# A planned graph network kernel: loads on ScalarE's queue, a third layer's product in three passes, one addition on GpSimd alone

## The chip, the cores and the metric

The kernel runs on one core of one Trainium2 chip. The metric is device microseconds of one execution, the median of several runs. The changed kernel is compared with the kernel before on the same inputs. Engine names in the profile: PE is TensorE (matmuls), PEld is its weight load, DVE is VectorE, ACT is ScalarE, POOL is GpSimd, SP is SyncE, which only issues transfers. PEq, ACTq, SPq and so on are the queues of instructions of these engines. L992 is line 992 of the kernel.

## The reference, cut to what matters

There are 128 graphs of 128 nodes with 256 features each, and an adjacency matrix of 0 and 1 for each graph. Four layers follow each other. Each normalises x, takes the positive part, computes a graph layer and adds the result to x.

```python
h = relu(layernorm(x))
# layer 0: three steps of a gated recurrent cell, the weights shared by the steps but for weight[i]
for i in range(3):
    aggr = A^T @ (h @ weight[i])                  # A = (adj != 0)
    gi, gh = aggr @ w_ih.T + b_ih, h @ w_hh.T + b_hh
    r, z = sigmoid(gi_r + gh_r), sigmoid(gi_z + gh_z)
    n = tanh(gi_n + r * gh_n)
    h = (1 - z) * n + z * h
x = x + h
# layer 1: for each relation r, (adj == r) @ h @ weight[r], summed, plus a bias
# layers 2 and 3: graph attention
e = leaky_relu(ei[:, None] + ej[None, :], 0.2)    # ei, ej: two projections of h @ W
x = x + softmax(where(adj, e, far)) @ (h @ W)
```

All arrays are float32. Adjacency values above 1 would need more than one relation in layer 1. The kernel holds a second program for that case and picks one at run time; with these inputs it takes the program for values 0 and 1.

## The kernel before

**Groups.** The work goes in 32 groups of four graphs (`G = 4`, `NG = 32`). A tile of one group is 128 partitions by 512 columns. Several groups are in flight at once, and x of a group is read twice, once for layer 0's normalisation (`load`, L529) and once at the last step of layer 0 (`fetch` at L1090), because only three buffers hold x. The adjacency tile is read three times for a group: at `load`, as its transpose (L1095), and in `again` (L522) for the masks of layers 2 and 3.

**Layer 0.** For each step, `step` (L940) forms three float32r pieces of h and of the aggregate (`forms`, L948): a rounded high part (L955 on ACT or L957 on DVE), a low part (L961, DVE), and their difference (`difference`, L468, on POOL or DVE). The gates are then sums of matmuls of 128x512 (`products`, L985, matmul L992) in three passes; between the second and the third pass the bank in PSUM is scaled by 1 + 2^-12 (`rescale`, L1003: L1013 on ACT or L1011 on DVE; L1005 scales with a bias). L1023 and L1040 are the tanh of the gates, L1035 to L1048 the elementwise updates on DVE. The new h is turned by `turn` (L478): a transpose in 32x32 blocks on DVE (L490), a write to DRAM (L493) and four reads back (L502). After the last step, two tiles of h are added to x (`residual`, L1078), on DVE or on POOL, whichever the planner finds free.

**Layers 1 to 3.** `product` (L792) computes a pair of graphs: first the sums over neighbours (`sums`, L761, matmul L765), then the product with the weights. A layer named in `THIN` does the second part in float32r in three passes: the sums are rounded to a high part (L806 on ACT, L808 on DVE), a low part follows (L811, DVE), a difference (L470), two passes (L819), a scale of the bank (L828 on DVE, L830 on ACT) and the third pass (L819). The three pieces lie in one set of buffers, `cform`. A layer that is not in `THIN` copies the sums (L461, on ACT or DVE) and does a plain float32 product (`mix`, L771, matmul L775). The last two groups (`PLAIN = 2`) are always plain. Before the change `THIN` is `(1, 2)`: the weights of layer 3, `wa_1`, are kept as plain float32 and those of layers 1 and 2 in three pieces, made at the start by `split` (L573). In the profile both `wa_0` and `wa_1` are written `wa`, since buffer numbers are left out.

**The start.** Weights come in, are split into pieces (L580 to L586) and, for layer 0, multiplied together (L598). All adjacency tiles are read once (L668) and their maximum taken (L670) to choose the program; all engines branch at L1236.

**What sets the order.** A planner (`Plan`, L172) records every operation with its engine or choice of engines, a cost, and the buffers it reads and writes. `order` (L215) then plays the operations forward in its own time: of those that can start on an engine soonest it takes the one with the lowest rank, and for an operation with two engines it settles which one. A rank is made of the group's due time (`PERIOD`, `CLOSE`), the length of the way behind the operation, and a number of its own from the table `OFFSETS`, one for each place in the code and stage. `LAG`, `HOP`, `OWN` and the argument `late` say when a result is seen by another engine. The order that comes out is fixed in the program; every engine works through its own list in order, and an instruction that waits holds those behind it.

Transfers are planned like operations of the engine that issues them. In the kernel before all of them but the first four weights are issued by SP:

```python
op("SP", dma(256), lambda g2=g2: nc.sync.dma_start(
    out=xt.t[:, 2 * g2 : 2 * g2 + 2, :],
    in_=x[ds(gi * G + 2 * g2, 2)].rearrange("g n d -> n g d")),
   w=[(xt, {2 * g2, 2 * g2 + 1})], after=after)
```

Transfers of both queues take turns with eight completion semaphores, so each also waits for the one eight issues before it.

Of the kernel before, what the change touches and what calls it, by code (L numbers as in the profile page):

```python
# [15 lines left out]
ALU = mybir.AluOpType  # L16
AX = mybir.AxisListType

P = 128
D = 256  # L20
KC = D // P
G = 4
T = G * P
# [15 lines left out]
OWN = {"PE": 0, "ACT": 125, "DVE": 125, "POOL": 80, "SP": 2500, "ACTQ": 2500}  # L39
PERIOD = 29902  # L40
CLOSE = 7183
CLOSING = 2
SOON = -210
# [3 lines left out]
LINE, SPREAD = 0, -1000  # L47
GIVE = -400
TAKE = -2500
TENSOR = ()  # L50
BLOCK = 32
NEAR = 69
# [12 lines left out]
THIN = (1, 2)  # L65
# [11 lines left out]
def act(n, ptrs=0):  # L77
    return 50 + 95 * ptrs + 0.833 * n


def dve(n):
    return 68 + n / 0.96


def dma(kb):
    return 470
# [3 lines left out]
    0: (-70252, -12514, 2287, 8809, -26238, -146194, 10750, 55634, 30994, -54821, -2879, -215, -254,),  # L90
    1: (-77596, -18751, -40109, -33244, -13055, -53723, -68528, 1773, -34806, -135119, 879, -98768, 51856,
        44795, -64452, -2716,),
    2: (-95804, -20611, 70568, -66959, -6282, -38365, 6331, 7167, -87557, -120685, 144159, 0, -60172, 22200,
        253, 2907, 38047,),
    3: (-102445, -23990, 38859, 16506, -38395, -77755, 61821, 576, 58832, 37279, 38392, 48590, -137270, -161,
        -4329, 88294, -5659, -1511, -24936, -35483,),
    4: (9420, 6970, 96990, 45577, 14137, -3081, -28597, -108133, -850, -77398, -8748, -81, 24213, -39147,
        5274, -117520, -39070, 4328, 73461, 2677, -9322, 38218,),
    5: (-53063, -10484, 13614, 9709, -9223, 0, 86360, -49387, 3891, -79089, 22834, -12125, 42, -143071,
        -20815, -7001, 39402, 8197, 210921, 979, -8129, 55104, -109511, 178418, -171023, -17919, -45955,  # L100
        32785, 202299, 15929, -75290, -16189,),
    6: (-8401, 1876, 0, -2867, -17545, -54409, -177384, 6635, -4173, 16809, 64025, 1422, -41374, 3498, 7298,
        112681, -960, 0, -167733, 3047, -20901, 48681, -50794, 104147, -14530,),
    7: (2011, -43268, -7473, -2193, -13120, 17374, 10030, 24727, -8835, -59753, 29500, -32772, -10542,
        -85496, -6214, -47593, 4322, -5746, -43839, -101654, -3101, 9392, -18883,),
    10: (31340, 140410, 166041, 86764, 86271, -82403, 47762, 173067, 157481, -33091, 90840, -8460, 85813,),
    11: (-90811, -5747, -11338, -10756, 2168, -27498, -36330, -9110, 13623, -65824, 59954, -36485, 65854,
        102114, -39462, 10659,),
    12: (-88894, -2718, 120398, -47746, 16864, -33143, 17060, 25017, -58235, -111482, 170409, 89873, -65258,
        61044, 3422, 23111, 49690,),  # L110
    13: (-59071, 17894, 109447, 41927, -4268, -51312, 111328, 77067, 108356, 88471, 46360, 263340, -35253,
        23414, 79162, 211888, 10834, -10383, 74698, 67176,),
    14: (-32758, 12684, 122607, -43352, -20519, -34186, -56784, -88737, -18648, -122741, -24236, -29303,
        31876, -49287, -17477, -128202, -71886, 71670, 64769, 11212, -103569, -34527,),
    15: (-186417, -106904, -40789, -64266, -8033, -13445, 16411, -115394, -129609, -221523, -34547, -153159,
# [258 lines left out]
def kernel(  # L374
# [20 lines left out]
    nc = tc.nc  # L395
# [28 lines left out]
    def build(general):  # L424
# [3 lines left out]
        op = plan.op  # L428
# [49 lines left out]
        def turn(nm, srcs, dst=None, w=None):  # L478
# [27 lines left out]
            return w  # L506

        state = {}

        def fetch(gi, name, after=()):  # L510
            xt = Buf(xs, f"{name}{gi}")
            for g2 in range(G // 2):
# [772 lines left out]
```

## Time and profile before

| what | value |
|---|---|
| median of 3 runs | 2353.08 us (2349.69 to 2353.46) |
| profiled execution, its own time | 2353.06 us |
| its span, first to last instruction | 2351.2 us |
| granted TensorE clock, mean | 0.996 |
| bytes moved over the span | 270.36 MB, 115 GB/s |
| matmuls of layer 0's gates (L992) | 6912 |
| issues on SP's queue: x loads, adjacency loads | 128; 96, and 32 more for the maximum |

In the lines of the profile's groups, the order is: line, engine, operation, tile written and tiles read, shapes, count; then busy time in us, mean length of one in ns; then the idle time just before them, and what ended most of it. In a line of waits, the numbers are the total in us, how many times, and the longest. In a timeline they are the start in us and the length. A busy sum of a TensorE line counts the time in which one of its matmuls was under way; neighbouring lines overlap.

### The profile page before, as it was taken

What the parts mean: (1) busy time and instruction counts of PE and PEld (TensorE: products, weight loads), DVE (VectorE), ACT (ScalarE), POOL (GpSimd) and SP (SyncE); (2) the same over time, 40 slices, a digit from 0 to 9 for tenths busy, and PEclk for the clock granted to TensorE, in tenths of its full rate; (3) what the DMA queues carried; (4) which work ended last, traced back from release to release, by engine and by line L of the source; (5) the groups of instructions that cost most, each with busy time, mean ns of one, the idle gap of its engine ahead of it and who ended that gap; (6) DMA issues with size and microseconds to landing.
All of it is one profiled execution on the core that took longest, in us unless ns stands there. A gap on an engine that the chain in (4) does not pass through costs nothing.

```text
span 2351.2 us, 39064 instructions
## 1 busy us (share of the span) xinstructions
PE 2291.9 (97%) x12137; PEld 1947.2 (83%) x12137; DVE 1978.2 (84%) x5405; ACT 1582.0 (67%) x3272; POOL 912.4 (39%) x729
## 2 busy tenths in 40 slices
PE   7999999999999999999999999999999999999997
PEld 6788888888888888888888888888888888788885
DVE  7858888888888888888888888888888888888887
ACT  6566676766676666666666766666766666666665
POOL 2334334443334443334343334343334343344421
PEclk9999999999999999999999999999999999999999
DMA  8535445555445455455455455455554555545431
GB/s 249 143 83 110 96 90 124 117 128 116 102 110 125 111 133 113 100 117 117 114 126 118 107 115 115 114 129 116 108 115 112 118 122 109 128 103 118 105 77 43
DMA packets 951273, 270.36 MB, mean 115 GB/s; under 512 B 677008, under 2 KB 939280, under 8 KB 951056
## 3 DMA queue, kind: packets, MB, share of 16 engines
q1 hardware_dynamic: 949968, 266.72, 50.0%
q8 instruction: 99, 1.62, 0.3%
q14 instruction: 118, 0.97, 0.2%
q10 hardware_dynamic: 1088, 1.05, 0.1%
HBM read 168.96 MB, written 98.69 MB: 114 GB/s over the span
## 4 chain that ended last, share of the span: by engine, by line
PE 64%; DVE 14%; DMA 10%; ACT 6%; SPq 4%; issue 3%; DVEq 0%; POOL 0%; ACTq 0%
PE bank L992 40%; PE bank L819 7%; PE bank L765 6%; PE bank L974 5%; PE bank L775 5%; DMA swap<-big 4%; SPq L502 4%; DMA big<-swap 3%; DVE junk L1119 3%; DVE form L961 2%; DMA wide<-swap 2%; ACT big L743 1%; DVE wide L1042 1%; DVE wide L1045 1%; DVE big L490 1%
## 5 line engine op out<-in xcount | busy, mean ns | idle before, releaser
L992 PE MATMUL bank<-form,wh_s 128*128 128x512 f32 x3456 | 953.4, 396 | 8.7 <-ACT bank L1005 4.6
L992 PE MATMUL bank<-form,wi_s 128*128 128x512 f32 x3456 | 944.0, 393 | 1.6 <-ACT bank L1013 0.9
L470 POOL TENSOR_TENSOR form<-form,form 128x512 fp32r<-128x512 f32 x383 | 517.7, 1362 | 800.4 <-DVE form L961 565.0
L992 PEld LDWEIGHTS bank<-form,wi_s 128*128 128x128 f32 x3456 | 644.1, 188 | 143.6 <-ACT bank L1013 3.1
L992 PEld LDWEIGHTS bank<-form,wh_s 128*128 128x128 f32 x3456 | 631.8, 188 | 151.5 <-ACT bank L1005 15.8
L1013 ACT ACTIVATE bank<-bank 128x512 f32<-128x512 f32 x448 | 255.4, 574 | 325.7 <-PE bank L992 324.4
L722 POOL TENSOR_TENSOR small<-small,nhalf 128x4 f32<-128x4 f32 (+2 forms) x140 | 142.2, 1020 | 408.8 <-DVE small L720 338.9
L1119 DVE CUSTOM_DVE_ANT_0 junk<-big,ub 128x256 bf16<-128x256 f32 x512 | 244.5, 478 | 14.2 <-ACT big L743 0.5
L743 ACT ACTIVATE big<-xs,small 128x256 f32<-128x256 f32 x384 | 200.1, 590 | 21.6 <-DVE small L726 12.2
L696 DVE BATCH_NORM_STATS2 small<-xs 128x6 f32<-128x256 f32 x512 | 190.0, 415 | 7.3 <-DMA xs<-in_x_dram 6.0
L470 POOL TENSOR_TENSOR cform<-cform,cform 128x512 fp32r<-128x512 f32 x120 | 155.2, 1294 | 96.2 <-DVE cform L811 83.0
L490 DVE STREAM_TRANSPOSE big<-wide 128x512 f32<-128x512 f32 x252 | 173.1, 697 | 4.0 <-ACT wide L743 2.3
L1035 DVE SCALAR_TENSOR_TENSOR bank<-big,bank 128x512 f32<-128x512 f32 x192 | 131.9, 690 | 48.5 <-PE bank L992 35.9
L955 ACT ACTIVATE form<-wide 128x512 fp32r<-128x512 f32 x179 | 109.2, 626 | 83.7 <-DMA wide<-swap 43.4
L1179 ACT ACTIVATE big<-big,small 128x128 f32<-128x128 f32 x256 | 99.8, 392 | 70.0 <-DVE small L1173 69.7
L1023 ACT ACTIVATE bank<-bank,b_rz 128x512 f32<-128x512 f32 x192 | 123.4, 655 | 34.0 <-PE bank L992 30.1
L1210 DVE SCALAR_TENSOR_TENSOR xs<-bank,small,xs 128x256 f32<-128x256 f32 x256 | 118.4, 475 | 31.6 <-PE bank L775 23.0
L1042 DVE TENSOR_TENSOR wide<-wide,bank 128x512 f32<-128x512 f32 x192 | 126.9, 682 | 21.4 <-ACT bank L1040 21.1
L765 PE MATMUL bank<-big,big 128*128 128x128 f32 x1024 | 130.7, 277 | 11.9 <-DVE wide L1045 7.1
L1023 ACT ACTIVATE big<-bank,b_rz 128x512 f32<-128x512 f32 x192 | 130.1, 681 | 16.3 <-PE bank L992 12.1
L765 PEld LDWEIGHTS bank<-big,big 128*128 128x128 f32 x1024 | 123.1, 192 | 19.4 <-DVE wide L1045 9.9
L974 PE MATMUL bank<-adjs,big 128*128 128x128 f32 x1024 | 131.2, 276 | 6.4 <-DMA big<-swap 5.1
(105 smaller groups left out, 3297.5 us busy)
## 6 DMA issues: line engine op xcount, KB each, us to landing
swap<-big SPq DMA_DIRECT2D x312, 256.0 KB, 2.5
big<-swap SPq DMA_DIRECT2D x992, 64.0 KB, 2.3
xs<-in_x_dram SPq DMA_DIRECT2D x128, 256.0 KB, 3.1
adjs<-in_adj_dram SPq DMA_DIRECT2D x64, 256.0 KB, 3.4
wide<-swap SPq DMA_DIRECT2D x128, 128.0 KB, 3.6
big<-line SPq DMA_DIRECT2D x60, 256.0 KB, 3.9
out_dram<-xs SPq DMA_DIRECT2D x30, 512.0 KB, 3.1
big<-in_adj_dram SPq DMA_DIRECT2D x32, 256.0 KB, 4.0
```

Of the source, the lines that this page charges most:

```text
L470: (nc.gpsimd if eng == "POOL" else nc.vector).tensor_tensor(at(df), at(lo).bitcast(F32), at(hi).bitcast(F32), ALU.subtract)
L490: nc.vector.transpose(part.t, src())
L696: op("DVE", dve(D), lambda g=g: nc.vector.bn_stats(s.t[:, ST + 6 * g : ST + 6 * g + 6], xt.t[:, g, :]), r=[(xt, {g})], w=[(s, {("mv", g)})])
L743: nc.scalar.activation(place(g), xt.t[:, g, :].rearrange("p (k m) -> p k m", k=KC), AF.Relu, bias=s.t[:, MR + g : MR + g + 1], scale=s.t[: ...
L765: nc.tensor.matmul(ps.t[:, (len(gs) * k + j) * P : (len(gs) * k + j + 1) * P], hs[g // 2].t[:, (g % 2) * D + k * P : (g % 2) * D + (k + 1) ...
L819: nc.tensor.matmul(po.t[:, j * D : (j + 1) * D], fs[f].t[:, (len(gs) * k + j) * P : (len(gs) * k + j + 1) * P], w.t[:, f, k, :], start=(st ...
L974: nc.tensor.matmul(pg.t[:, g * P : (g + 1) * P], of()[:, g * P : (g + 1) * P], flags(m0)[:, g * P : (g + 1) * P], start=True, stop=True,)
L992: nc.tensor.matmul(ps.t, w.t[(slice(None), *row, j, k, slice(c * P, (c + 1) * P))], b.t, start=(start and x == 0), stop=(x == len(terms) - ...
L1013: nc.scalar.mul(ps.t, ps.t, by)
L1023: op("ACT", act(T, 1), lambda: nc.scalar.activation(to.t, ps.t, AF.Tanh, bias=b_rz.t[:, c : c + 1], scale=0.5), r=[b_rz, *([ps] if kept el ...
L1042: op("DVE", dve(T), lambda c=c, ps=ps: nc.vector.tensor_tensor(hT.t[:, c, :], hT.t[:, c, :], ps.t, ALU.subtract), r=[ps], w=[(hT, {c})])
L1119: nc.vector.tensor_tensor_reduce(out=junk.t, in0=part, in1=ub[i].t[:, v, :], op0=ALU.mult, op1=ALU.add, scale=1.0, scalar=0.0, accum_out=s ...
```

## The change

1. The loads of x and of the adjacency tiles are issued by ACT's queue (`QUEUE = "ACT"`, new function `arrive`); weights, turns, rows of the attention, the reads for the maximum and the stores stay on SP.
2. `THIN` takes in layer 3: its weights are split at the start, and its products go in three passes.
3. The last h is added to x on POOL alone.
4. The planner's numbers are new: an issue costs 530 ns instead of 470 (`ISSUE`), a load on ACT is seen 4400 ns late (`LANDING`), a transfer's own delay `OWN` on SP is 4500 instead of 2500, the costs of `act` and `dve` are some ns higher, `PERIOD`, `CLOSE`, `SOON`, `NEAR`, `GIVE`, `TAKE`, `LINE` and `SPREAD` change, and every number of `OFFSETS`. So every engine's order changes, and which of ACT and DVE does an operation that both can do.

```diff
-OWN = {"PE": 0, "ACT": 125, "DVE": 125, "POOL": 80, "SP": 2500, "ACTQ": 2500}
-PERIOD = 29902
-CLOSE = 7183
+OWN = {"PE": 0, "ACT": 125, "DVE": 125, "POOL": 80, "SP": 4500, "ACTQ": 2500}
+PERIOD = 36849
+CLOSE = 17602
...
-SOON = -210
+SOON = 295
...
-LINE, SPREAD = 0, -1000
-GIVE = -400
-TAKE = -2500
+LINE, SPREAD = -1800, -1400
+GIVE = -2500
+TAKE = -2600
...
+ISSUE = 530
+LANDING = 4400
+QUEUE = "ACT"
...
-NEAR = 69
+NEAR = 19
...
-THIN = (1, 2)
+THIN = (1, 2, 3)
...
-    return 50 + 95 * ptrs + 0.833 * n
+    return 57 + 95 * ptrs + 0.833 * n
...
-    return 68 + n / 0.96
+    return 74 + n / 0.96
...
-    return 470
+    return ISSUE
...
-                op("SP", 470, give, r=[part], w=[(swap, {k})], late=GIVE)
+                op("SP", ISSUE, give, r=[part], w=[(swap, {k})], late=GIVE)
...
-            op("SP", 470 * P // BLOCK, take, r=[swap], w=[w], late=TAKE)
+            op("SP", ISSUE * P // BLOCK, take, r=[swap], w=[w], late=TAKE + 800 * (n - 1))
...
+        def arrive(dst, src, w, after=()):
+            on_act = QUEUE == "ACT"
+            op(QUEUE, dma(256), lambda: (nc.scalar if on_act else nc.sync).dma_start(out=dst(), in_=src), w=w,
+               after=after, late=LANDING if on_act else 0)
...
-                op("SP", dma(256), lambda g2=g2: nc.sync.dma_start(
-                    out=xt.t[:, 2 * g2 : 2 * g2 + 2, :],
-                    in_=x[ds(gi * G + 2 * g2, 2)].rearrange("g n d -> n g d")),
-                   w=[(xt, {2 * g2, 2 * g2 + 1})], after=after)
+                arrive(lambda g2=g2: xt.t[:, 2 * g2 : 2 * g2 + 2, :],
+                       x[ds(gi * G + 2 * g2, 2)].rearrange("g n d -> n g d"), [(xt, {2 * g2, 2 * g2 + 1})], after)
...
-                    def residual(eng, k=k, h=h):
+                    def residual(k=k, h=h):
                         part = xt.t[:, :, k * P : (k + 1) * P]
-                        (nc.gpsimd if eng == "POOL" else nc.vector).tensor_tensor(
-                            part, part, h.t.rearrange("p (g d) -> p g d", g=G), ALU.add)
-
-                    op(("DVE", "POOL"), (dve(T), 1250), residual, r=[h], w=[(xt, set(range(G)))], port=True)
+                        nc.gpsimd.tensor_tensor(part, part, h.t.rearrange("p (g d) -> p g d", g=G), ALU.add)
+
+                    op("POOL", 1250, residual, r=[h], w=[(xt, set(range(G)))], port=True)
```

The adjacency loads in `again`, in `load` and before layer 1 change to `arrive` in the same way; the cost of `terms` (L1125) goes from 850 to 880.

## The prediction

> **What bounds the kernel now.** I read the page's engine totals first, then the busy time in stretches of one period in the middle of the run, then the chain that ended last, then the costs by kind and form, and last the queues and the start.
>
> ```profile
> span 2351.2 us, 39064 instructions
> PE 2291.9 (97%) x12137; PEld 1947.2 (83%) x12137; DVE 1978.2 (84%) x5405; ACT 1582.0 (67%) x3272; POOL 912.4 (39%) x729
> ```
> ```profile
> 1019.30:1090.00 70.70, 70.51 (x378) 60.02 (x377) 61.55 (x165) 48.25 (x101) 28.19 (x23) 1.00 0.53 116
> 1090.00:1160.00 70.00, 69.72 (x377) 59.93 (x377) 60.36 (x165) 48.35 (x101) 28.04 (x23) 1.00 0.52 117
> ```
> After each stretch stand its length and the busy time of PE, PEld, DVE, ACT and POOL, then the granted clock. TensorE is busy 70.5 of 70.7 us and 69.7 of 70.0 us, at full clock. One group of four graphs passes every 70.4 us or so (12 periods from 1019.34 to 1867.22 us: 70.66 each). ACT leaves 22 us of each period free, POOL 42, DVE 9 to 10. So TensorE's own work sets the pace; all 59.3 us of its idle time lie at the ends and in small holes (15.2 us before 60 us, 17.0 after 2280, some 27 between).
>
> The chain gives TensorE's pace as starts that do not overlap (start, length, what):
>
> ```profile
> 1064.38 1.73 PE bank L775 x8
> 1066.10 0.93 PE bank L819 x8
> 1067.04 1.73 PE bank L775 x8
> 1068.76 0.47 PE bank L819 x4
> ```
> L775 is a plain layer 3 product of a pair of graphs: eight records, 1.73 us. L819 is the three-pass form that layers 1 and 2 use: 8 records (two passes) in 0.93 us, 4 (the third) in 0.47.
>
> ```profile
> L470 POOL TENSOR_TENSOR cform<-cform,cform 128x512 fp32r<-128x512 f32 x120 | 155.2, 1294 | 96.2 <-DVE cform L811 83.0 <-DVE small L710 6.8 <-DVE small L711 4.3
> L811 DVE SCALAR_TENSOR_TENSOR cform<-cform,bank 128x512 fp32r<-128x512 f32 x120 | 81.4, 679 | 5.0 <-ACT cform L806 4.9
> L830 ACT ACTIVATE bank<-bank 128x512 f32<-128x512 f32 x97 | 56.6, 583 | 62.0 <-PE bank L819 61.9
> L1080 DVE TENSOR_TENSOR xs<-xs,big 128x512 f32<-128x512 f32 x47 | 40.9, 870 | 69.6 <-DMA big<-swap 66.5 <-issue 3.1
> L1080 POOL TENSOR_TENSOR xs<-xs,big 128x512 f32<-128x512 f32 x13 | 17.1, 1315 | 25.0 <-DMA big<-swap 21.1 <-ACT big L1179 2.8 <-DVE form L961 1.0
> ```
> Here the mean length (ns) after each busy sum prices what is added and moved.
>
> **The change part by part.** Counts are from the order of instructions in the two built programs, first branch of the If (the inputs take it).
>
> **Layer 3 in three passes.** 60 pairs (30 groups; the last two groups keep the plain form) lose 1.73 us and gain 0.93 + 0.47 = 1.40: 60 x 0.33 = 19.8 us less on TensorE, all on the path that sets the end. The busy sums would give less: L775 with wa is 120.8 us for 512 records, of which 480 go (113 us), against 107.6 us for the 720 of L819 with wa, hence 5.7. But those sums overlap at every change of line (the PE rows together pass 2291.9 us by far), so I take the chain's starts and keep 5.7 as the low end. The other engines pay: 60 of L811 (0.679) = 41 us on DVE and 60 differences (1.294) = 78 us on POOL. The copy of the pair's sums becomes the rounding, and one rescale per pair is new.
>
> **What the planner moves between ACT and DVE.** ACT: +77 rescales of the product (0.583) = 44.9, +87 of L1013's kind (0.574) = 49.9, +15 roundings (0.595) = 8.9, -24 of L955 from wide (0.626) = -15.0, -13 copies (0.586) = -7.6, rest some 4: +85 us. DVE: +41 above, -87 L1011 (0.695) = -60.5, -47 copies (0.663) = -31.2, +45 roundings (0.682) = 30.7, -17 rescales (0.700) = -11.9, +24 roundings from wide (0.423) = 10.2, -47 residuals (0.870) = -40.9: -61 us with small change. DVE falls to about 1917 us (82%).
>
> **The last h added by GpSimd alone.** 47 adds leave DVE (above), with the 66.5 us that DVE stood waiting for the turned h before them; POOL gains 47 x 1.315 = 61.8 us and those waits, and ends at 912 + 78 + 62 = 1052 us (45%). A rule speaks against this: the Trainium skill, GPSIMD Engine Reference, section 3.1 "Elementwise — side-by-side cycle accounting", keeps elementwise work on DVE and has a tensor_tensor 1.96 times slower on GpSimd. The rows here say 1315 against 870 ns, 1.5 times. On the path that would be 47 x 0.445 = 21 us by the row and 47 x 0.835 = 39 us by the rule (an estimate from that page's ratio). I take nothing, since POOL's 42 free us per period hide 2 x 1.3 us. If that cover is gone, what is late next is layer 1's normalisation (it reads x) and, on POOL's own queue, the differences behind the add, for which TensorE's third passes wait.
>
> **Loads issued by ScalarE.** 224 issues (7 per group: 128 halves of x, 96 adjacency tiles) leave SP's queue and enter ACT's. An issue took 0.48 us on ACT's queue at the start (1.57 for the next three), so about 0.5: 112 us more on ACT, which ends near 1582 + 85 + 112 = 1779 us, 76%; in a period 48.3 + 2.7 + 3.5 = 54.5 of 69.8. The Trainium skill, DMA: Bandwidth & Descriptors, section "Issuing engines are not separate DMA queues", says that a second issuing engine saves the sequencer's time only. SP's queue spends some 0.4 to 0.5 us on each of 1861 issues, under 900 of 2351 us, and TensorE waited 9.0 us in all for turned data (5.1 at L974, 3.9 at L765). A reading of the second queue as more bandwidth could at most claim those 9 us; by the rule it is 0, and I take 0.
>
> The danger is the waits that come along. On SP they were:
>
> ```profile
> SPq L513 <- ACT wide L743: 120.6, 54, 8.9
> SPq L513 <- DMA out_dram<-xs: 69.9, 25, 4.4
> ```
> In before, the x load stands right behind the store that empties its buffer (TensorE work of 0.89 us between them in program order), and SP alone stood 2.8 us each time. On ACT's in-order queue everything behind would stand too: the rescales L1013 first, then TensorE. The new order puts 8.45 us of TensorE work between store and load in nearly every middle group, against 0.43 us issue + 3.1 landing. Each load also waits for the transfer eight issues back, since eight completion semaphores go round; the shortest such distance in a middle group is 3.46 us, to a swap read that lands in 2.3. The first row's wait, for ACT's own reading of x, costs nothing on ACT but its pipeline's end. So in the middle I cost the loads at nothing, hidden by ACT's 15 free us per period; without that cover each issue is 0.5 us.
>
> **The start.** There the cover is missing. ACT's queue now begins with 15 issues before its first table load (4 weights among 11 loads), and the last waits for a transfer eight back.
>
> ```profile
> 2.84 1.28 ACT L580 ACT_TABLE_LOAD   x1 [2.84 <-issue]
> 8.38 0.38 ACT L580 ACTIVATE wi_s<-bank 128x256 fp32r<-128x256 f32 x1 [4.25 <-PE bank L598]
> ```
> ```profile
> 15.89 0.43 SPq L531 DMA_DIRECT2D adjs<-in_adj_dram  x1
> 44.17 1.28 PE L992 MATMUL bank<-form,wh_s 128*128 128x512 f32 x4
> ```
> In before ACT splits weights from 8.38 us, with gaps; the fifth adjacency load (now ACT's last) was issued at 15.89. So ACT would begin at 15 to 17 us. Before the first L992 product it then has 78 splits at 0.305 (their starts when back to back), 8 normalisations at 0.49 and 6 roundings at 0.53, some 31 us: first product at 47 to 48 against 44.17. Range of the delay: 0 (other engines set it) to 8 (all of ACT's late start); I take 4 us. The verdict on adj comes at an earlier point of the work; TensorE lost 0.8 us at 80 to 100 us, so I give it 0. The end is alike (39.3 us of TensorE work behind the last product before, 38.7 after): 0, with 5 us either way.
>
> **Sum.** 2351.2 - 19.8 + 4 = 2335.4 us of span; the profiled execution took 2353.06, 1.9 more than its span, so 2337. That execution equals the median of the runs (2353.08), so no correction.
>
> **Rivals.** (1) ACT waits behind its loads and the kernel gets slower. Place: one load per group meets its transfer late; price: the 2.8 us seen on SP, of which half reaches TensorE behind the late rescale: 31 x 1.4 = 43 us, 2380. It decides from 0.5 us per group (15.8 / 31). For it: 324.4 us of ACT's idle time end on TensorE's products, so rescales run close behind them. Against it: the distances above. (2) POOL becomes late: the add waits for turned h (4.2 us each on POOL before, 21.1 / 5), and a difference behind it comes late; if 0.2 us of each of 60 reaches TensorE, +12 us: 2349. Against: POOL has over half its time free. (3) The gain on TensorE is only the busy sums' 5.7 us: 2353.1 - 5.7 + 4 = 2351, no change. Against: four chain starts that repeat in the next period.
>
> **How the numbers follow.** All hidden 0.65 (2337, own range 2328 to 2346: the start's 0 to 8 and the end's 5); rival 1 0.20; rival 2 0.09; rival 3 0.06. The measurement tells 0.2% (4.7 us) from no change. Faster: 0.64 of the first, 0.05 of rival 2, 0.02 of rival 1 and 0.01 of rival 3: 0.72. Same: 0.01, 0.03, 0.01, 0.04: 0.09. Slower: 0.19. The range 2326 to 2366 leaves out the bulk of rival 1 above and small chances below.
>
> **What would show it.** Right: a period near 69.8 us with TensorE over 99% busy in it; L819 with wa at 1440 records, L775 with wa near 32; ACT near 76%, DVE 82, POOL 45; first L992 product at 46 to 49 us; waits of the loads on ACT's queue that total a few us. Wrong: a period above 70.7 us, with L1013 or the loads at the head of ACT's waits (rival 1), or third passes that wait for POOL's differences (rival 2), or a first product after 52 us.

## The result, and the profile after

| what | before | after |
|---|---|---|
| median of 5 runs | 2353.08 us (2348.95 to 2353.62) | 2362.19 us (2360.86 to 2364.31) |
| ratio after to before, 95% interval | | 1.0046 [1.0032, 1.0061] |
| span of the profiled execution | 2351.2 us | 2362.4 us |
| granted TensorE clock, mean | 0.996 | 0.988 |

The change makes the kernel 0.46% slower. The forecast was 2337 us; 2362 lies inside the range, on the other side of no change.

In the changed kernel the lines have moved: L992 is now L998, L819 L825, L775 L781, L765 L771, L974 L980, L490 L495, L493 L498, L502 L507, L668 and L670 L674 and L676, L470 L475, L811 L817, L830 L836, L1080 L1086, L1013 L1019. All loads of x and adjacency have the one line L517 (`arrive`).

The page's totals of the changed kernel:

```profile
span 2362.4 us, 39704 instructions
PE 2283.8 (97%) x12377; PEld 1943.5 (82%) x12377; DVE 1959.9 (83%) x5338; ACT 1655.7 (70%) x3422; POOL 1045.0 (44%) x836
```

Busy time by stretch, two periods in the middle (columns as in the prediction), and pieces of the chain that ended last, from the first of them:

```profile
1010.12:1080.13 70.01, 69.48 (x386) 59.32 (x385) 59.77 (x162) 50.88 (x104) 33.24 (x27) 1.00 0.51 117
1080.13:1150.00 69.87, 69.87 (x388) 59.96 (x388) 60.06 (x164) 50.86 (x104) 33.48 (x27) 1.00 0.53 118
```
```profile
1010.12 7.32 PE bank L998 x32
...
1076.04 0.93 PE bank L825 x8
1076.97 0.91 PE bank L998 x4
1077.88 0.89 PE bank L771 x8
1078.77 0.47 PE bank L825 x4
```

Groups by form:

```profile
L475 POOL TENSOR_TENSOR cform<-cform,cform 128x512 fp32r<-128x512 f32 x180 | 244.7, 1360 | 212.2 <-DVE cform L817 167.6 <-DVE small L717 20.0 <-DVE small L716 8.6
L825 PE MATMUL bank<-wa,cform 128*128 128x256 f32 x1440 | 218.2, 287 | 2.0 <-ACT bank L836 1.4 <-DVE cform L817 0.4
L817 DVE SCALAR_TENSOR_TENSOR cform<-cform,bank 128x512 fp32r<-128x512 f32 x180 | 121.8, 677 | 24.7 <-ACT cform L812 24.0
L1086 POOL TENSOR_TENSOR xs<-xs,big 128x512 f32<-128x512 f32 x60 | 78.2, 1303 | 22.4 <-DMA big<-swap 22.2
```

Everything that the change was to do, it did. A pair of the three-pass form costs 0.93 + 0.47 us, the two periods take 69.9 us on average instead of 70.66, TensorE is busy in over 99% of them. The loss is elsewhere, and a busy share of 97% in both kernels doesn't show it: a TensorE at a lower clock is busy too.

**A ledger of TensorE.** To find the place, I price every matmul by its start-to-start length at full pace, as the chains give it: 0.229 us for 512 columns (7.32 / 32), 0.117 for a record of L825 (0.93 / 8), 0.216 for a plain one of 256 columns (1.73 / 8), 0.111 for 128 columns (0.89 / 8). The sum is the work. What time passed beyond the work is lost: idle, or slow. Work falls from 2239.5 to 2220.1 us (-19.4), the loss rises from 111.7 to 142.4 us (+30.7), and together that is +11.3 us, the difference of the spans (11.2; the medians differ by 9.1, since the profiled execution was the changed kernel's longest of five). TensorE's idle time alone rises by 19.3 us, from 59.3 to 78.6; the rest of the loss is work at less than full pace.

| stretch | lost before, us | lost after, us | predicted difference | measured |
|---|---|---|---|---|
| 0 to 100 us | 27.8 | 46.8 | +4 | +19.0 |
| 100 to 2000 | 46.9 | 47.1 | 0 | +0.2 |
| 2000 to the end | 37.0 | 48.5 | 0, with 5 either way | +11.5 |

The start, by stretch (columns as above), first before, then after. The granted clock is the number after POOL's count:

```profile
40.00:60.00 20.00, 18.97 (x76) 14.94 (x75) 17.57 (x39) 10.79 (x25) 8.21 (x7) 0.89 0.82 232
60.00:80.00 20.00, 19.42 (x82) 14.85 (x81) 19.67 (x34) 12.38 (x23) 2.83 (x2) 1.00 0.73 212
```
```profile
40.00:60.00 20.00, 12.25 (x49) 9.85 (x50) 17.78 (x42) 13.28 (x37) 6.46 (x5) 0.74 0.81 212
60.00:80.00 20.00, 12.97 (x57) 10.20 (x55) 19.42 (x34) 9.16 (x15) 1.89 (x2) 0.88 0.91 292
```

In these 40 us TensorE ran 158 matmuls before and 106 after. The timelines of the changed kernel on ACT and TensorE (start, length; in brackets the idle time before, and its releaser) say where it waits:

```profile
18.01 1.28 ACT L586 ACT_TABLE_LOAD   x1 [18.01 <-DMA adjs<-in_adj_dram]
...
54.39 2.17 PE L998 MATMUL bank<-form,wh_s 128*128 128x512 f32 x4 [4.51 <-ACT form L961]
...
81.63 2.17 PE L998 MATMUL bank<-form,wh_s 128*128 128x512 f32 x4 [8.66 <-ACT form L961]
```

ACT's first own work comes at 18.0 us (2.8 before), the first gate product at 54.4 us (44.2 before), and the first product of the second group waits 8.7 us more.

The waits of TensorE for turned data (total, times, longest), before and then in the changed kernel, and the waits of SP's queue in the changed kernel:

```profile
PE bank L974 <- DMA big<-swap: 5.1, 8, 1.5
PE bank L765 <- DMA big<-swap: 3.9, 6, 1.6
```
```profile
PE bank L771 <- DMA big<-swap: 19.9, 21, 3.6
PE bank L980 <- DMA big<-swap: 7.3, 7, 2.5
```
```profile
SPq L498 <- DVE big L495: 572.9, 174, 15.1
SPq L507 <- DMA swap<-big: 345.5, 183, 4.7
...
SPq L498 <- DMA adjs<-in_adj_dram: 17.0, 18, 4.6
```

TensorE waits for turned data three times as long as before (27.2 against 9.0 us). The last row is the new one; SP's list before has no wait of L493 for a load. SP, about to write a turned part, stands until an adjacency load has landed, with which that write shares no data.

### The profile page after: what moved, and what is told of

The parts are those of the page before. It is cut to its first block, busy times and chain, and to the rows that moved or that the text cites. A ratio compares the mean times of both kernels' runs of the same rounds, so it can differ in the third digit from the quotient of the medians.

```text
span 2362.4 us, 39704 instructions
## 1 busy us (share of the span) xinstructions
PE 2283.8 (97%) x12377; PEld 1943.5 (82%) x12377; DVE 1959.9 (83%) x5338; ACT 1655.7 (70%) x3422; POOL 1045.0 (44%) x836
## 4 chain that ended last, share of the span: by engine, by line
PE 81%; DMA 7%; DVE 5%; ACT 2%; SPq 2%; issue 1%; ACTq 0%; DVEq 0%
PE bank L998 57%; PE bank L825 9%; PE bank L771 7%; PE bank L980 7%; DMA big<-swap 3%; DMA swap<-big 3%; SPq L507 2%; PE bank L781 1%; DVE junk L1123 1%; DVE big L495 1%; DVE form L967 1%; ACT big L1170 0%; DMA big<-in_w0T_dram 0%; DVE most L676 0%; DVE wide L1051 0%
## 5 line engine op out<-in xcount | busy, mean ns | idle before, releaser
L998 PE MATMUL bank<-form,wh_s 128*128 128x512 f32 x3456 | 952.8, 396 | 13.2 <-ACT form L961 13.2
L998 PE MATMUL bank<-form,wi_s 128*128 128x512 f32 x3456 | 952.3, 396 | 0.0
L475 POOL TENSOR_TENSOR form<-form,form 128x512 fp32r<-128x512 f32 x383 | 503.7, 1329 | 748.6 <-DVE form L967 713.1
L998 PEld LDWEIGHTS bank<-form,wi_s 128*128 128x128 f32 x3456 | 641.6, 189 | 139.3 <-ACT bank L1019 5.4
L998 PEld LDWEIGHTS bank<-form,wh_s 128*128 128x128 f32 x3456 | 626.0, 189 | 129.7 <-ACT form L961 14.4
L1019 ACT ACTIVATE bank<-bank 128x512 f32<-128x512 f32 x535 | 310.3, 580 | 329.5 <-PE bank L998 327.6
L475 POOL TENSOR_TENSOR cform<-cform,cform 128x512 fp32r<-128x512 f32 x180 | 244.7, 1360 | 212.2 <-DVE cform L817 167.6
L728 POOL TENSOR_TENSOR small<-small,nhalf 128x4 f32<-128x4 f32 (+1 forms) x140 | 141.2, 1013 | 249.6 <-DVE small L726 180.8
L1123 DVE CUSTOM_DVE_ANT_0 junk<-big,ub 128x256 bf16<-128x256 f32 x512 | 228.9, 447 | 17.9 <-ACT big L749 3.0
L702 DVE BATCH_NORM_STATS2 small<-xs 128x6 f32<-128x256 f32 x512 | 193.6, 415 | 43.4 <-POOL xs L1086 35.6
L825 PEld LDWEIGHTS bank<-wa,cform 128*128 128x128 f32 x1440 | 195.5, 189 | 35.1 <-issue 17.5
L825 PE MATMUL bank<-wa,cform 128*128 128x256 f32 x1440 | 218.2, 287 | 2.0 <-ACT bank L836 1.4
L495 DVE STREAM_TRANSPOSE big<-wide 128x512 f32<-128x512 f32 x252 | 173.9, 700 | 5.8 <-PE bank L604 1.7
L771 PEld LDWEIGHTS bank<-big,big 128*128 128x128 f32 x1024 | 126.7, 197 | 34.5 <-issue 25.4
L771 PE MATMUL bank<-big,big 128*128 128x128 f32 x1024 | 133.0, 284 | 20.7 <-DMA big<-swap 19.9
L967 DVE SCALAR_TENSOR_TENSOR form<-form,wide 128x512 fp32r<-128x512 f32 x192 | 146.4, 776 | 5.0 <-ACT form L961 2.0
L1046 ACT ACTIVATE bank<-bank,bih_s 128x512 f32<-128x512 f32 x192 | 124.3, 653 | 37.4 <-PE bank L998 37.4
```

The source lines that it names most:

```text
L475: (nc.gpsimd if eng == "POOL" else nc.vector).tensor_tensor(at(df), at(lo).bitcast(F32), at(hi).bitcast(F32), ALU.subtract)
L495: nc.vector.transpose(part.t, src())
L702: op("DVE", dve(D), lambda g=g: nc.vector.bn_stats(s.t[:, ST + 6 * g : ST + 6 * g + 6], xt.t[:, g, :]), r=[(xt, {g})], w=[(s, {("mv", g)})])
L728: op("POOL", 1000, lambda: nc.gpsimd.tensor_tensor(columns(RS), columns(RS), nhalf.t[:, gs.start : gs.stop], ALU.pow), r=[nhalf], w=[own(" ...
L771: nc.tensor.matmul(ps.t[:, (len(gs) * k + j) * P : (len(gs) * k + j + 1) * P], hs[g // 2].t[:, (g % 2) * D + k * P : (g % 2) * D + (k + 1) ...
L825: nc.tensor.matmul(po.t[:, j * D : (j + 1) * D], fs[f].t[:, (len(gs) * k + j) * P : (len(gs) * k + j + 1) * P], w.t[:, f, k, :], start=(st ...
```

## The experiments

All runs keep the planned order of their base, except where it says otherwise. The runs came in four sets, each on one chip of its own with the kernel before beside them, which took 2344.64 us in the first set (e1, e2, e6, e7), 2364.55 in the second (e8, e9, e10, e14), 2343.91 in the third (e2b, e11, e12, e13) and 2361.71 in the fourth (e1b, e15, e16). So ratios to the kernel before in the same set are compared. Times and losses of single profiles are compared within a set, apart from the start, whose loss hardly differs between sets. A loss is that of one execution, which can lie some us off the median of its kernel; where the two differ, the ratio counts.

The theories: A, ACT's queue is held at the start by its 15 issues. B, the planned order of the start is what costs. C, the loads on ACT cost in the middle, and then either D2, because SP waits for them, or E, because issuing takes ACT's time. D was the opposite, that a queue of their own helps.

**The loads, first and later, in both orders.** In the changed kernel the first 11 loads go back to SP (e1), or all 224 (e2); in the kernel before the first 11 go to ACT (e6), or all the others (e7).

The edit of e1 (e2 has `nc.sync` there for every load), and that of e7, in which `gi < 3` and `gi < 5` mark the first loads as in e1 (e6 has the two engines exchanged):

```diff
-            op(QUEUE, dma(256), lambda: (nc.scalar if on_act else nc.sync).dma_start(out=dst(), in_=src), w=w,
+            op(QUEUE, dma(256), lambda: (nc.sync if early else nc.scalar).dma_start(out=dst(), in_=src), w=w,
...
+                       name == "x0_" and gi < 3)
...
+                    adj[ds(gi * G, G)].rearrange("g i j -> i g j"), [ai], (), gi < 5)
```
```diff
+        def on(early):
+            return nc.sync if early else nc.scalar
...
-                op("SP", dma(256), lambda g2=g2: nc.sync.dma_start(
+                op("SP", dma(256), lambda g2=g2: on(name == "x0_" and gi < 3).dma_start(
...
-            op("SP", dma(256), lambda: nc.sync.dma_start(
+            op("SP", dma(256), lambda: on(gi < 5).dma_start(
```

> The changed kernel, with the same planned order, but the first eleven loads (x of the first three groups, the adjacency of the first five) issued by SP; all later loads stay on ACT. Theory A (the start: ACT's queue is held by these loads until 18 us, and everything behind follows): ACT's table load comes near 3 us, the first product of the gates at 45 to 48 us instead of 54.4, and 10 to 16 us of the 19 that the start lost come back: 2346 to 2352 us. Rival B (the planned order of the start is the fault: the second group's turn stands behind 24 reads for the maximum, whoever issues the loads): the wait of TensorE of 8.7 us at 73 to 82 us stays and no more than 5 us come back: 2357 to 2362 us.

> The changed kernel, with the same planned order, but all 224 loads issued by SP. Theory A: in the middle the loads cost ACT nothing that matters, so it agrees with the run in which only the first eleven moved, within 3 us: 2345 to 2354 us. Rival C (the loads cost in the middle too, as rescales come 0.5 us late behind an issue): it is 10 us or more faster than that run, with a period under 69.6 us. Rival D (the loads on a queue of their own help, as turns no longer stand behind a load that waits): it is 5 us or more slower than that run.

> The kernel before, with its own planned order, but the first eleven loads issued by ACT. Theory A: ACT starts its splits at 14 to 19 us, the first product comes 5 to 10 us later than at 44.2, and the time rises by 5 to 15 us: 2358 to 2368 us. Rival B: the start is set by the order elsewhere; the time stays within 3 us of 2353.

> The kernel before, with its own planned order, but all loads except the first eleven issued by ACT, so the x load stands on ACT right behind the store that empties its buffer (0.89 us of TensorE's work between them). By the prediction's first rival each group's wait of 2.8 us on ACT reaches TensorE by half or more: 31 x 1.4 = 43 us, near 2396 us. If ACT's free time takes it up, the time stays within 10 us of 2353.

| kernel | time, us | ratio to before, 95% | lost 0 to 100 | 100 to 2000 | 2000 to end |
|---|---|---|---|---|---|
| e1, changed, first loads on SP | 2352.42 | 1.0032 [1.0023, 1.0041] | 42.0 | 43.4 | 48.8 |
| e2, changed, all loads on SP | 2339.95 | 0.9978 [0.9969, 0.9987] | 42.4 | 30.0 | 43.9 |
| e6, before, first loads on ACT | 2348.59 | 1.0012 [1.0002, 1.0022] | 30.1 | 40.7 | 38.0 |
| e7, before, later loads on ACT | 2358.96 | 1.0051 [1.0033, 1.0069] | 27.8 | 51.3 | 41.9 |

The same edit has much the same price in both orders. The later loads on ACT cost 0.54% in the new order (e1 to e2, 12.5 us) and 0.51% in the old one (e7, four runs); the first loads cost 0.12% in the old order, and in the ledger 2 to 5 us. All loads on ACT cost some 15 us in either order. The rest of the change, e2, is 0.2% faster than before. C stands, and D falls. At the start e1 and e6 came out as B had them and not as A: with no load on ACT at all, 42.4 us are still lost by 100 us, against 27.8 in the old order. A's part is there all the same: the first gate product comes 4.3 us later in e6 than before (48.48), and 5.9 us earlier in e1 than in the changed kernel (48.50), of which 2 to 5 us reach the loss. The waits of TensorE in e1, where it is L772 and L981, and in e2 show what the later loads had done:

```profile
PE bank L772 <- DMA big<-swap: 17.1, 20, 3.8
PE bank L981 <- DMA big<-swap: 7.2, 8, 2.4
```
```profile
PE bank L998 <- ACT form L961: 12.5, 2, 9.5
PE bank L771 <- DMA big<-swap: 6.0, 13, 1.2
PE bank L980 <- DMA big<-swap: 3.1, 3, 1.9
```

TensorE's waits for turned data fall from 24.3 to 9.1 us, 15.2 of the 18 us by which the losses of these two profiles differ. SP's waits of L498 for adjacency, 15.8 us in e1, are gone in e2. The start's long wait (L998 for L961) stays. In e7, the old order, TensorE waits 16.4 us for turned data and not 9.0, and SP's reads of turned data stand 9.0 us for adjacency loads, in four waits of up to 4.3 us, for which they don't stand before.

**Which loads, and is it ACT's time?** In the second set: all adjacency loads on SP and the 122 later x loads on ACT (e8), and the mirror, 91 later adjacency loads on ACT and all x loads on SP (e9). e10 belongs to another question and is also the base here, since all its loads are on SP.

First the edit from e1 to e8, then that to e9:

```diff
-                    adj[ds(gi * G, G)].rearrange("g i j -> i g j"), [ai], after)
+                    adj[ds(gi * G, G)].rearrange("g i j -> i g j"), [ai], after, True)
...
-                    adj[ds(gi * G, G)].rearrange("g i j -> i g j"), [ai], (), gi < 5)
+                    adj[ds(gi * G, G)].rearrange("g i j -> i g j"), [ai], (), True)
...
-                    adjT[ds(gi * G, G)].rearrange("g i j -> i g j"), [aiT], late)
+                    adjT[ds(gi * G, G)].rearrange("g i j -> i g j"), [aiT], late, True)
```
```diff
-                       name == "x0_" and gi < 3)
+                       True)
```

> The changed kernel in its own planned order; all loads of adjacency (adj, adjT) and the first x loads are issued by SP, the other 122 x loads stay with ACT. Theory D2 (in the middle SP stands for completion of ACT's adjacency loads: 17.0 us in 18 waits in the changed kernel, none over 2.2 us for x loads; and TensorE then waits for turned data): most of the 12.5 us between the kernel with all loads on SP and the one with only the first there comes back, 8 us or more: ratio to before 0.998 to 0.9995; SP's waits for adjs vanish and TensorE's wait for big<-swap at the recurrent line of the first layers falls from 17 us to 8 or less. Rival E (each issue costs ACT's time, whatever it loads): the gain goes by number of issues, 96 of 224, so 5 us: ratio 1.001.

> The mirror: all x loads and the first adjacency loads are issued by SP, the other 91 adjacency loads stay with ACT. Theory D2: little comes back, 0 to 4 us: ratio 1.0015 to 1.0035, SP's waits for adjs stay near 15 us. Rival E: 7 us come back by number of issues: ratio about 1.000.

e8: 2361.83 us, ratio 0.9993 [0.9985, 1.0001]. e9: 2366.56 us, 1.0009 [1.0000, 1.0017]. With no load on ACT, e10 has 0.9978 [0.9968, 0.9988] there. So the 91 adjacency loads cost about 0.31% and the 122 x loads about 0.15%: an adjacency load is near three times as dear, which speaks for D2, and in e8 SP's waits for adjacency at L498 are gone, as D2 had it. But e9 gave more back than D2 had it, which E had near right (1.000), and in these profiles TensorE's wait for turned data at L772, the later L771, is 23 us in both, not 8. That part of the expectation was missed. These two profiles can't carry much: each is of the shortest execution of its kernel, e9's 7 us under its median, and e8, e9 and e10 lose the same in theirs. And e10, without any load on ACT, also waits 20.2 us there. In e9 SP's waits for adjacency did not stay near 15 us either:

```profile
SPq L498 <- DMA adjs<-in_adj_dram: 8.4, 2, 5.2
```

Of 18 waits two long ones are left, and the small ones went with the x loads. What does tell e8 and e9 apart is one place. Between 250 and 300 us e9 loses 7.7 us, e8 1.1, e10 2.1; e1 had lost 6.2 there, e2 0.9, the changed kernel 7.1.

Then ACT's time alone, beside e2 once more (e2b): ScalarE makes two small copies, 0.43 us together, at the place of each of 209 later loads, while SP issues the load. This adds work that the reference doesn't need.

```diff
+            def both():
+                nc.sync.dma_start(out=dst(), in_=src)
+                if state.get("open"):
+                    for _ in range(2):
+                        nc.scalar.copy(state["open"].t, ident.t[:, 0 : F])
...
```

> All loads on SP, and at the planned place of each load after the branch (209 of 224) ScalarE copies 32 columns twice, about 0.4 us, as long as it takes to issue a load; these copies wait for no buffer and no transfer. Theory D2 (SP's standing for ACT's loads costs the 12.5 us, not ACT's time): within 3 us of the kernel with all loads on SP. Rival E (ACT's time is what costs): 8 to 12 us slower than it.

> The kernel with all loads on SP once more, as the base for the other three on this chip: ratio 0.9978 again, within 0.001.

e13: 2339.39 us, 0.9982 [0.9972, 0.9992]. e2b: 2339.43 us, 0.9985 [0.9978, 0.9991]. No difference, though ACT is busy 67 us longer in the profile (1723.7 against 1656.5): E falls. What costs in a load on ACT is not the time in which ACT issues it.

**One load of 213.** The place between 250 and 300 us in the changed kernel, timelines of ACT's and SP's queues and of TensorE:

```profile
281.73 0.58 ACT L1019 ACTIVATE bank<-bank 128x512 f32<-128x512 f32 x1 [0.50 <-PE bank L998]
281.74 0.37 ACTq L517 DMA_DIRECT2D adjs<-in_adj_dram  x1
```
```profile
275.96 4.13 SPq L507 DMA_DIRECT2D big<-swap  x8
284.79 0.38 SPq L498 DMA_DIRECT2D swap<-big  x1
287.13 1.90 SPq L507 DMA_DIRECT2D big<-swap  x4
```
```profile
290.87 3.76 PE L771 MATMUL bank<-big,big 128*128 128x128 f32 x16 [3.64 <-DMA big<-swap]
```

The load of group 5's adjacency is behind a rescale L1019 in ACT's list, which waits for TensorE, so it is issued at 281.74 and lands 2.99 us later, at 284.73. SP was through with its reads at 280.09. Its write L498 goes at 284.79, 0.06 us after the landing. In the built program that write is the eighth transfer after the load and waits for the completion semaphore that the load counts up. The turned data are 4.7 us late, TensorE stands 3.6 us and then takes 3.76 us for 16 matmuls that take 2.02 in e16. In e16 this one load goes to SP; e1b, which is e1 again, is its base in the same set.

```diff
-                    adj[ds(gi * G, G)].rearrange("g i j -> i g j"), [ai], (), gi < 5)
+                    adj[ds(gi * G, G)].rearrange("g i j -> i g j"), [ai], (), gi < 6)
```

> As the changed kernel with its first loads on SP, and of the 213 later loads one more goes to SP: group 5's first adjacency load, whose landing at 284.73 us let SP's write of a turned part go at 284.79 in the changed kernel. Theory D2 (SP waits for that load's completion semaphore, TensorE then idles 3.6 us at 290.9 and runs slowly for some us): the loss between 250 and 300 us, 6.2 us with the first loads alone on SP and 7.1 in the changed kernel, falls to 0.5 to 2; about 5 us in the time, ratio 0.2% below the other one of this call. Rival E (it is the number of loads on ACT): one load of 213 changes nothing, 6 us stay.

> The kernel with the first loads on SP once more, as the base on this chip: ratio 1.0032 within 0.001, loss between 250 and 300 us about 6 us.

e16: 2361.35 us, 1.0003 [0.9991, 1.0016]. e1b: 2365.82 us, 1.0023 [1.0012, 1.0034]. The medians differ by 4.5 us; the loss between 250 and 300 us falls from 6.5 to 1.9. The same place in e16, SP's queue and TensorE, and TensorE's in e1b:

```profile
279.73 0.44 SPq L498 DMA_DIRECT2D swap<-big  x1
...
285.17 0.51 SPq L517 DMA_DIRECT2D adjs<-in_adj_dram  x1
```
```profile
286.53 2.02 PE L772 MATMUL bank<-big,big 128*128 128x128 f32 x16
```
```profile
288.29 3.57 PE L772 MATMUL bank<-big,big 128*128 128x128 f32 x16 [4.09 <-DMA big<-swap]
```

SP writes as soon as its reads are out, the load follows at 285.17, nobody waits. That settles D2 for this place: about a third of what the later loads cost is one load. SP's waits of L498 for adjacency, in e1b and in e16:

```profile
SPq L498 <- DMA adjs<-in_adj_dram: 18.3, 19, 4.9
```
```profile
SPq L498 <- DMA adjs<-in_adj_dram: 11.9, 17, 1.1
```

The long wait went and the short ones stayed. For these and SP's other waits for loads, which make the rest, D2 is the likely cause but not shown one by one.

**GpSimd's addition.** All loads on SP as in e2, and the last h added by DVE at the same place of the order.

```diff
-                        nc.gpsimd.tensor_tensor(part, part, h.t.rearrange("p (g d) -> p g d", g=G), ALU.add)
+                        nc.vector.tensor_tensor(part, part, h.t.rearrange("p (g d) -> p g d", g=G), ALU.add)
```

> All loads on SP, and the last h added to x by DVE at the same place of the planned order (GpSimd before). My costing of this part at nothing: within 2 us of the kernel with all loads on SP, ratio 0.997 to 0.9985. Rival P (GpSimd's add is late for the norm that follows, DVE waits 43 us for it in the changed kernel): at least 3 us faster, ratio below 0.9965.

2359.79 us, 0.9978 [0.9968, 0.9988], the ratio of e2, in another set. It costs nothing, as taken, though DVE waits 35.6 us for it at L702 in the changed kernel.

**The start's order.** The second group's turn stood behind 24 reads of the scan in SP's list (52.9 to 70.7 us in the changed kernel), so I held the scan for the cause. e14 moves the turn and the last reductions in e2's list; e11 leaves 24 of the 32 pieces of the scan out of e2, and e12, the control, out of the kernel before. In e14's edit the numbers are places in the list ahead of the branch: the first of a pair is moved behind the second.

```diff
+MOVES = (
+    (339, 252), (342, 254), (349, 264), (257, 275), (364, 320), (366, 325), (367, 329), (368,
+    331), (370, 332), (375, 335), (356, 346), (358, 346), (360, 346), (362, 346), (365, 346),
+    (371, 346), (373, 346), (376, 346), (399, 385), (403, 391), (407, 394),
+)
```
```diff
+            read = f < 8
-            op("SP", dma(256), lambda part=part, f=f: nc.sync.dma_start(
+            op("SP", dma(256), lambda part=part, f=f, read=read: read and nc.sync.dma_start(
...
-            op("DVE", dve(T), lambda part=part, f=f: nc.vector.tensor_reduce(
+            op("DVE", dve(T), lambda part=part, f=f, read=read: read and nc.vector.tensor_reduce(
...
```

> All loads on SP; in the part before the branch the second group's last transpose, its write and its turned read stand ahead of the scan's later pieces, and its splits ahead of the first group's close; the last 7 reductions of the scan are drawn forward. Theory B (the start's loss is the planned order: the second group's first product waits 9.5 us for its turned h): that product starts at 68 to 71 us and not 77.8; 6 to 10 us faster than with all loads on SP, ratio 0.9935 to 0.9955. Rival V (the verdict of the scan, at 86.3 us, holds the branch, and the time is waited there): nothing gained, ratio 0.9975 to 0.9985.

> All loads on SP, and of the scan of adjacency that chooses the branch only 8 of 32 pieces are read and reduced (the other 24 reads by SP and 24 reductions by DVE are left out). Theory B (at the start the second group's turn stands behind the scan in SP's and DVE's order): the second group's first product no longer waits (9.5 us with the whole scan), the loss by 100 us falls from 42 to 33 or less, 8 to 13 us faster than with all loads on SP: ratio 0.992 to 0.9945. Rival (the scan is only cover for a wait on something else, such as the rounding of the weights): within 3 us, ratio 0.9965 to 0.998.

> The kernel before with the same 24 pieces of the scan left out, as the control. Theory B: its planned order has no such wait, so 0 to 4 us faster: ratio 0.9983 to 1.000. If it gains 8 us or more as well, the scan costs both orders alike and doesn't explain the difference.

e14: 2368.76 us, 1.0023 [1.0013, 1.0032]. It got slower: with the turn ahead, SP's scan reads came later, DVE stood 10.4 us for them, and the first group's turned h for its next layer came so late that TensorE stood 13.1 us at L994:

```profile
91.14 2.05 PE L994 MATMUL bank<-adjs,big 128*128 128x128 f32 x8 [13.09 <-DMA big<-swap]
```

e11: 2341.24 us, 0.9995 [0.9986, 1.0004]; e12: 2341.85 us, 0.9994 [0.9982, 1.0005]. Leaving the scan out gains nothing in either order; in e11 the second group's product still waits 7.8 us, and 42.2 us are lost by 100 us. So my theory of the scan fell. e11 left the next place bare: SP's write of the second half waits for DVE's transpose, and DVE's list has that transpose behind the first group's update (L1049 there), which waits, by way of ACT, for TensorE's products of that group (timeline of DVE in e11):

```profile
67.43 0.69 DVE L1049 TENSOR_TENSOR wide<-wide,bank 128x512 f32<-128x512 f32 x1 [5.68 <-ACT bank L1047]
68.03 0.70 DVE L495 STREAM_TRANSPOSE big<-wide 128x512 f32<-128x512 f32 x1
```

e15 moves that in e11: the transpose, its write and its read ahead, the splits after them, and TensorE's next adjacency products of the first group behind four gate products of the second. 24 of 32 pieces of the scan are left out, as in e11.

```diff
+MOVES = (
+    (339, 252), (342, 254), (349, 264), (364, 320), (366, 325), (367, 329), (368, 331), (370,
+    332), (375, 335), (379, 406), (382, 406), (386, 406), (389, 406), (393, 406), (394, 406),
+    (396, 406), (399, 406), (403, 406), (404, 406),
+)
```

> As with all loads on SP and the short scan (24 of 32 pieces of the scan left out), and in the part before the branch the second half of the second group's turn (DVE's transpose, SP's write and turned read) stands ahead of the first group's close, its splits follow the first group's products at once, and TensorE takes the second group's first four gate products ahead of the first group's next adjacency products. Theory B2 (what keeps the second group's first product is DVE's order: its transpose stands behind the first group's close, which waits for TensorE; the scan itself, left out, changed nothing): that product starts at 68 to 70 us and not at 76.7, and the loss by 100 us falls from 42.2 to 34 to 38: ratio 4 to 8 us better than 0.9995, so 0.996 to 0.998. Rival (the next bound is as near: the first group's turned h for its next layer, landed at 81): the loss by 100 us stays above 40 and the ratio above 0.9985.

2353.70 us, 0.9969 [0.9958, 0.9980], against 0.9995 for e11 in another set. TensorE in e11 and in e15:

```profile
76.73 2.17 PE L999 MATMUL bank<-form,wh_s 128*128 128x512 f32 x4 [7.76 <-ACT form L962]
```
```profile
69.20 1.08 PE L1013 MATMUL bank<-form,wh_s 128*128 128x512 f32 x4
...
79.00 2.04 PE L995 MATMUL bank<-adjs,big 128*128 128x128 f32 x8 [3.73 <-DMA big<-swap]
```

The second group starts at 69.2 us without a wait, and the ratio came as B2 had it. But the loss by 100 us falls only to 39.9, short of the 34 to 38 expected: the next wait, the first group's turned h, is right behind. TensorE stands 3.7 us for it and goes on at half pace (2.04 us for eight matmuls that take 1.06 in e11). So B2 had two marks of three, and its rival's reason was there too. Of the start's 14 us in the order, some 2 by the ledger are tied to DVE's place for that transpose; the ratio would give 6 us, but over two sets and the whole run. The rest is spread over the order of the first 80 us (the first gate product alone is at 48.9 us in e2, against 44.2 before) and stays open.

**The version to keep.** e2, the changed kernel with its loads on SP, beats the kernel before in both sets that have it, 0.9978 [0.9969, 0.9987] and 0.9985 [0.9978, 0.9991], and so the changed kernel, which has 1.0046 in its own.

## Why the prediction was wrong

The span was to fall by 15.8 us and rose by 11.2, 27 us off. Some 11 us of that are the loads, which cost some 15 us against the 4 forecast. Some 15 are the rest of the change: -20 us forecast, and -0.2% or some 5 us measured in e2, since the new order's losses at the start and the end, taken at nothing, eat most of the gain.

**"60 x 0.33 = 19.8 us less on TensorE": right.** The chain's lengths (0.93 and 0.47) and the 1440 records came as said. The ledger's 19.4 is built from the same lengths and proves nothing by itself; the period does, which fell by some 0.7 us (70.66 to 69.9), where 19.8 us over 30 groups ask for 0.66. The low end of 5.7 from the busy sums, rival 3, would be 0.2 a period and is out.

**The other engines: near enough.** DVE 1959.9 us was forecast near 1917, 2% too low; POOL 1045.0 against 1052. ACT is 1655.7 busy and spends 84 us on issues, which the page doesn't count as busy: 1740 against 1779, since an issue on ACT took 0.375 us (median of 224) and not 0.5. None of them sets the pace. GpSimd's addition at nothing held (e10), and TensorE idles only 2.0 us before the passes of L825 with `wa`, 1.8 of it put down to ACT and DVE; so rival 2 is out. (TensorE's idle time after 2280 us before is 16.2 us, not 17.0; nothing rests on it.)

**"So in the middle I cost the loads at nothing": this step failed.** I had the eight completion semaphores, and checked one direction: an ACT load that waits for one of SP's transfers eight back. The other direction I left out: an SP transfer that waits for one of ACT's loads eight back. SP's list is ahead of ACT's, whose load stands behind whatever ACT does before it, TensorE's products included; so SP, which feeds TensorE with turned data, is tied to ACT's pace. The later loads cost 12 to 13 us (e1 to e2, e7); that it is by this tie was shown for one load of 4.5 us. In the comparison of before and after it is hidden: 100 to 2000 us shows +0.2, since the new order with the loads on SP loses 5 to 10 us less there than the old one (30.0 in e2 and 40.7 in e6 in one set; 33.3 in e2b and 38.4 in e12 in another), and the loads give it back. That the forecast for the middle agrees with the ledger is luck: two unpriced terms cancel.

**"The start: I take 4 us": this failed too.** It measured 19. The first gate product came at 54.4 us, past the 52 that the prediction names as a sign of being wrong. The term that I worked out, ACT's late beginning, is there (18.0 us; 15 to 17 said) and measures 2 to 5 us, as e1, e2 and e6 have it. What I didn't price is the new planned order of the start itself: 14 us with no load on ACT. I had given it nothing since TensorE lost 0.8 us between 80 and 100 us in before; that says how well the old order covered its waits, and nothing of how well the new one would. The order of the two programs could have been read for a part of it: the second group's transpose behind the first group's close.

**"The end is alike: 0, with 5 us either way": it measured 11.5**, of which some 6 stay with all loads on SP (43.9 in e2, 38.0 in e6) and some 5 go with the loads (48.8 in e1). Equal work behind the last product didn't mean equal waits; which waits stayed was not tested.

**Rival 1** had the sign and not the mechanism. It said that ACT waits behind its loads, at 43 us. No such wait is near the head of ACT's waits outside the start, and ACT's time is free (e13). In e7, where the x load stands right behind the store, it asked for 43 us more than before, and 0.51%, some 12 us, came; that ACT's free time would take it up to within 10 us was just missed too. The loads cost some 15 us, by SP's waits where it was traced.

## What to carry to other kernels

Moving transfers to a second queue doesn't make two independent queues while both take completion semaphores in turn from one set, eight here: a list that runs ahead then waits for a list that runs behind. Look at both directions of that tie, and at what the later list stands behind. A gain on the bound engine is read in the middle of the run, but a new planned order must be priced at its start and end as well, stage by stage, and a ledger of work at full pace shows losses there that a busy share hides.

## What the runs showed of the hardware that was not expected

**A wait of TensorE is paid twice.** Stretches around the stall at 290.87 us in the changed kernel, cut where the clock changes; the granted clock is the number after POOL's count:

```profile
283.41:286.82 3.41, 3.41 (x16) 2.72 (x15) 3.29 (x7) 1.19 (x3) 2.54 (x3) 1.00 0.43 124
286.82:290.23 3.41, 0.41 (x2) 0.00 (x0) 2.44 (x12) 1.12 (x2) 1.18 (x2) 1.00 0.49 80
290.23:293.64 3.41, 2.77 (x13) 2.80 (x14) 0.34 (x1) 0.63 (x2) 0.00 (x0) 0.50 0.45 151
293.64:297.05 3.41, 3.41 (x12) 2.83 (x12) 1.38 (x2) 2.48 (x5) 2.51 (x2) 0.50 0.00 0
297.05:300.46 3.41, 3.41 (x21) 2.96 (x20) 2.29 (x4) 1.73 (x4) 1.29 (x1) 1.00 0.39 89
```

One stretch with 0.41 us of work in 3.41 is followed by half clock. The next, with 2.77 us of work, doesn't bring the clock back; the one after it, full of work, does. So 3.6 us of idling cost 3.6 us and then some 3.1 more, 6.2 us of work at half pace; the stretch from 250 to 300 us loses 7.1 us here and 1.9 in e16, where the wait is gone and the granted clock is 1.00. The Trainium skill, TensorE: Matmul & The Clock Gate, Part 1, says that the clock is halved after an idle window of about 3.4 us and restored after a busy one, and that the windows run on regardless of the kernel. The rows agree: the low stretch is two such windows, since the work began inside the first. In the two periods shown above TensorE's small holes leave the granted clock at 1.00. At the start it is the same as at the stall: the first gate products take 2.17 us for four matmuls in the changed kernel and 1.28 before.

**Chips differ where transfers are on the path.** e1 and e1b are one kernel on two chips. It took 2352.42 us on the chip where the kernel before took 2344.64, and 2365.82 where that took 2361.71. The reads of turned data land in 2.3 us (median) on the first and in 2.4 on the second, and TensorE's wait for them at L772 is 17.1 and 25.8 us. That the landing is what makes the times differ is likely, not shown.
